# Attention's front and side work: load order, wide first projections, GpSimd norms and splits, paced pieces

## The chip, the cores and the metric

The kernel runs on one core of a Trainium2 chip. A core has TensorE (PE; its weight loads, PEld, are listed apart), VectorE (DVE), ScalarE (ACT), GpSimd (POOL) and SyncE (SP), which here only issues transfers. Each engine works through its own queue in order and waits for others by semaphores. The metric is the device time of one execution in microseconds, lower is better.

## The reference, cut to what matters

Two blocks of attention and feed-forward follow one another on x of shape (4, 1024, 128). The change touches the first attention alone, and the place in it where the first feed-forward's input is prepared:

```python
x = x + _L0_attn_ref(_layernorm(x), ...)      # 16 heads of 8, B=4, S=1024, E=128
...
Q = x @ wq + bq                               # and K, V
Q = Q.reshape(B * H, S, D)                    # a plain reshape: 64 groups of 1024 rows of 8
scores = einsum('bqd,bkd->bqk', Q, K) / sqrt(D)
ctx = einsum('bqk,bkd->bqd', softmax(scores), V)
out = ctx.reshape(B, S, E) @ wo + bo + x
out = (out - mean) * rsqrt(var + 1e-5) * gamma + beta
```

The reshape cuts the row-major result without a transpose, so a group of "Q" is 64 consecutive tokens x 16 chunks of 8 features. 512 tokens (a "half") hold eight such groups, treated as two sets of four.

## The kernel before, in words

**Stages.** `tile_block` loads x (`load_x`: eight transfers of 256 KB on SP), runs `attention` (0 to about 1001 us of the profile), the first feed-forward, a gated linear attention and a mixture of experts. Everything from `attention` on the engines other than PE is put into its queue by a scheduler that takes the earliest-written instruction that its model holds ready and whose buffer is free; PE's order in the main loop is the written one (`manual_schedule`).

**Front.** `attention` loads the weights wq and wk, then the biases bq and bk by 32 small transfers on ACT's queue (16 copies each, L250), then wv, wo, bv and three broadcast rows, then all weights of the later stages (`load_later_weights`, which also has DVE compute `half_s`, L83, from a loaded vector). `prepare(0)` then does the first half at once.

**prepare(hf)**, for each of the eight halves of 512 tokens: statistics of four 128-token tiles on DVE (`norm_stats`; the power -1/2 runs on GpSimd, L196), the scaling of each tile on DVE (`norm_apply`, L200), xnb = xn + bo on GpSimd (L311), four transposes (L318) and a copy to xnT on ACT (L319), then eight projections, four for k and four for q, of four chunks each: 16 small products into the one bank "misc" (L328; the profile lists 32 passes), the bias by DVE (`raw`, L336), and the signed split: hi = raw x sign, rounded, on DVE (L345), raw x take and the sum on GpSimd (L346, L347). `hi` and `raw` have two buffers each. Last `values` writes v (L366).

**The main loop** runs 16 sets x 2 query halves x 8 key chunks x 2 steps = 512 steps. A step has a score tile in a double bank (two products, L586, and two with the negated maxima, L595), its exponential on ACT (`pr`, L603), and a maxima tile for a later set: two products (L396) into a double bank and a reduction on DVE (`nm`, L403). The double banks come from one pool of three. Every second step adds the weighted sum (L513). The maxima lead by ten pairs of steps. When half a set's maxima are done, `place` splits them, GpSimd writes them into `mxpad` (L422, L423), and PE transposes them (L413) for the score tiles.

**Side work.** `others()` is called at every other step and takes one entry from `after` (places; and of a finished set: normalize L446 to L456, project, output, residual) and one from `ahead` (the next half's `prepare`), at most one of them with a use of "misc". When `ahead` is empty it also emits one of eleven comparison pieces of half 1 (`compare_pieces`, L120 to L123): four GpSimd operations over 512 columns on buffers of the tags `hi` and `raw`, which check the later weights. `output` adds the residual input (y) and has DVE take the statistics; `residual` scales on DVE (z, L200), after the power on GpSimd, and GpSimd does gamma, beta and the sum into x. In the last half `ahead` holds instead `first_pieces` (norm and transposes of the first two blocks for the feed-forward, xn in a `raw` buffer), the turning of the weights, and a flag.

Of the kernel before, what the change touches and what calls it, by code (L numbers as in the profile page):

```python
# [24 lines left out]
class Block:  # L25
# [5 lines left out]
    def __init__(self, ctx: ExitStack, tc: tile.TileContext, ins, out):  # L31
        self.tc, self.nc, self.ins, self.out = tc, tc.nc, ins, out
        nc = self.nc
        self.const = ctx.enter_context(tc.tile_pool(name="const", bufs=1))
        self.xs = self.ctile([P, NT, E], "xs")
        self.ident = self.ctile([P, P], "ident")
        make_identity(nc, self.ident)
        self.mhalf = self.ctile([P, 16], "mhalf")
        nc.gpsimd.memset(self.mhalf, -0.5)
# [4 lines left out]
    def load_x(self, x):  # L44
        src = x.rearrange("b s e -> (b s) e").rearrange("(n p) e -> p n e", p=P)
        h = TPB // 2
        for n in range(0, NT, h):
            self.nc.sync.dma_start(self.xs[:, n : n + h, :], src[:, n : n + h, :])
# [105 lines left out]
    def first_pieces(self, work, bank):  # L154

        nc, out = self.nc, []
        for blk, x2 in enumerate(self.first_x):
            src = self.xs[:, 4 * blk : 4 * blk + 4, :]
            got = {}

            def norm(src=src, got=got):
                mv, rs = self.norm_stats(work, src, 4)
                got["xn"] = xn = work.tile([P, 4, E], F32, name="xn", tag="raw")
                for k in range(4):
                    self.norm_apply(xn[:, k, :], src[:, k, :], mv, rs, k)

            def turn(x2=x2, got=got):
                ps = bank()
                for k in range(4):
                    nc.tensor.transpose(ps[:, k * P : (k + 1) * P], got["xn"][:, k, :], self.ident)  # L170
# [3 lines left out]
            out += [(0, norm), (1, turn)]  # L174
        return out[0::2] + out[1::2]
# [9 lines left out]
    def norm_stats(self, pool, src, n):  # L185
# [11 lines left out]
        return mv, rs  # L197

# [17 lines left out]
    def attention(self):  # L216
# [7 lines left out]
        with ExitStack() as ctx:  # L224
# [13 lines left out]
            wpad = {}  # L238
            for key in ("wq", "wk"):
                nat = ct([P, NC, D], f"{key}_nat")  # L240
                nc.sync.dma_start(nat, ins[f"L0_attn_{key}"].rearrange("i (c d) -> i c d", d=D))
                wp = ct([P, NC, 4, D], f"{key}_pad")
                nc.vector.tensor_copy(wp, nat.unsqueeze(2).to_broadcast([P, NC, 4, D]))
                wpad[key] = wp.rearrange("p c r d -> p c (r d)")
            b4 = {"wq": ct([P, NC], "bq4"), "wk": ct([P, NC], "bk4")}
            for key, bkey in (("wq", "bq"), ("wk", "bk")):
                src = ins[f"L0_attn_{bkey}"].rearrange("(c d) -> d c", d=D)
                with nc.allow_non_contiguous_dma(reason="128 words"):
                    for j in range(16):
                        nc.scalar.dma_start(b4[key][D * j : D * j + D, :], src)  # L250
# [22 lines left out]
            for cl in range(2):  # L273
                nc.scalar.dma_start(
# [4 lines left out]
            )  # L279
            self.load_later_weights()  # L280
# [13 lines left out]
            def prepare(hf):  # L294
# [10 lines left out]
                def stats():  # L305
                    got["ln"] = self.norm_stats(work, x_h, NT2)

                def apply():
                    for n in range(NT2):
                        self.norm_apply(xn[:, n, :], x_h[:, n, :], *got["ln"], n)  # L310
# [10 lines left out]
                def project(key, c0):  # L321
                    bt["done"].add((key, c0))
                    ps = misc()
                    ps3 = ps.rearrange("p (c n) -> p c n", c=4)
                    xj = xnT.rearrange("p (i j t) -> p j i t", j=4, t=T)
                    for cc in range(4):
# [8 lines left out]
                    raw = work.tile([P, 4, NSET, T], F32, name="raw", tag="raw")  # L335
                    nc.vector.tensor_tensor(  # L336
                        raw,
                        ps3.rearrange("p c (i t) -> p c i t", t=T),
                        b4[key][:, c0 : c0 + 4].unsqueeze(2).unsqueeze(3)
                        .to_broadcast([P, 4, NSET, T]),  # L340
                        ALU.add,
                    )

                    hi = work.tile([P, 4, NSET, T], F32R, name="hi", tag="hi")
                    nc.vector.tensor_scalar(hi, raw, sign[key], None, ALU.mult)  # L345
# [6 lines left out]
                    )  # L352

# [19 lines left out]
                todo = [(0, stats), (0, apply), (1, turn)]  # L373
                for k in ("wk", "wq"):
                    todo += [(1, lambda k=k, c=c: project(k, c)) for c in range(0, NC, 4)]
                todo += [(1, values)]
                bt["done"] = set()
                return bt, todo
# [57 lines left out]
            def finish(hf, i, qh, oacc, ctok, xnb):  # L436
# [6 lines left out]
                def normalize():  # L443
# [5 lines left out]
                    ps4 = ps.rearrange("p (c j r) -> p c j r", c=4, r=32)  # L449
                    rc = work.tile([P, 4, 4], F32, name="rc", tag="rc")  # L450
                    nc.vector.reciprocal(rc, ps4[:, :, :, D])
                    cv = ctok.rearrange("p h (q c l d) -> p q l c h d", q=2, l=2, d=D)
                    for cl in range(2):
                        rows = slice(cl * T, (cl + 1) * T)
                        for jl in range(2):
                            nc.vector.tensor_tensor(  # L456
                                cv[jl * T : (jl + 1) * T, qh, cl],
                                ps4[rows, :, jl::2, 0:D],
                                rc[rows, :, jl::2].unsqueeze(3).to_broadcast([T, 4, 2, D]),
                                ALU.mult,  # L460
                            )
# [9 lines left out]
                def output():  # L471
# [16 lines left out]
                    got["y"] = y  # L488
                    got["ln"] = self.norm_stats(work, y, 2)

                def residual():
                    y = got["y"]
                    z = work.tile([P, 2, E], F32, name="z", tag="z")
                    for h in range(2):
                        self.norm_apply(z[:, h, :], y[:, h, :], *got["ln"], h)
                    n0 = hf * NT2 + 2 * i
                    xt = xs[:, n0 : n0 + 2, :]

                    def row(t):
                        return t.unsqueeze(1).to_broadcast([P, 2, E])  # L500

                    nc.gpsimd.tensor_tensor(z, z, row(gamma_b), ALU.mult)
                    nc.gpsimd.tensor_tensor(z, z, row(beta_b), ALU.add)
                    nc.gpsimd.tensor_tensor(xt, xt, z, ALU.add)

                evacuate()
                after.append((1, normalize))
                if qh:
                    after.extend([(1, project), (1, output), (0, residual)])
# [27 lines left out]
            for _, f in todo:  # L537
# [10 lines left out]
            def others():  # L548


                free = True
                for queue in (after, ahead):
                    if queue and (free or not queue[0][0]):
                        banks, f = queue.popleft()
                        f()
                        free = free and not banks
                if free and not ahead and compare:
                    compare.pop(0)()

# [1049 lines left out]
```

## Time and profile before

| | us |
|---|---|
| median of 4 runs | 1651.91 (1640.6 to 1666.95) |
| the profiled execution | 1656.16 |
| its span, first to last instruction | 1654.4 |
| mean granted TensorE clock | 0.926 |

| engine | busy us | share | instructions |
|---|---|---|---|
| PE | 1397.5 | 84% | 10256 |
| DVE | 1111.4 | 67% | 1870 |
| ACT | 841.9 | 51% | 1056 |
| GpSimd | 483.9 | 29% | 462 |

Busy shares are averages over the stages, and a busy PE isn't a PE at its peak. A row of the timeline gives start, duration, engine, line, operation, what is written <- what is read, and in brackets the engine's idle time before it with what ended it. A wait for several semaphores is put down to the one that came last. The granted clock is a record of changes between 1.0 and 0.5, with none before 56 us.

### The profile page before, as it was taken

What the parts mean: (1) busy time and instruction counts of PE and PEld (TensorE: products, weight loads), DVE (VectorE), ACT (ScalarE), POOL (GpSimd) and SP (SyncE); (2) the same over time, 40 slices, a digit from 0 to 9 for tenths busy, and PEclk for the clock granted to TensorE, in tenths of its full rate; (3) what the DMA queues carried; (4) which work ended last, traced back from release to release, by engine and by line L of the source; (5) the groups of instructions that cost most, each with busy time, mean ns of one, the idle gap of its engine ahead of it and who ended that gap; (6) DMA issues with size and microseconds to landing.
All of it is one profiled execution on the core that took longest, in us unless ns stands there. A gap on an engine that the chain in (4) does not pass through costs nothing.

```text
span 1654.4 us, 25028 instructions
## 1 busy us (share of the span) xinstructions
PE 1397.5 (84%) x10256; PEld 706.4 (43%) x10256; DVE 1111.4 (67%) x1870; ACT 841.9 (51%) x1056; POOL 483.9 (29%) x462
## 2 busy tenths in 40 slices
PE   2699893889899898898988998988884878679998
PEld 1343341334343343343433434665652544445554
DVE  3798793799797798897987854777663555622220
ACT  0066652566655566566656675466663322254332
POOL 4442069036061060240430003554550000202110
PEclk9789997899997899999999998999995887789999
DMA  5000000000000000000000000000000000101110
GB/s 142 3 1 2 1 2 0 1 2 1 1 2 1 1 2 1 1 2 1 1 2 1 1 1 1 1 1 1 1 0 2 1 1 1 34 5 51 51 52 14
DMA packets 23247, 16.06 MB, mean 10 GB/s; under 512 B 9536, under 2 KB 20432, under 8 KB 23120
## 3 DMA queue, kind: packets, MB, share of 16 engines
q1 hardware_dynamic: 15792, 7.99, 1.7%
q0 software_dynamic: 1920, 6.29, 1.3%
q8 instruction: 84, 1.38, 0.3%
q10 hardware_dynamic: 5408, 0.05, 0.2%
q14 instruction: 43, 0.35, 0.1%
HBM read 12.23 MB, written 2.10 MB: 9 GB/s over the span
## 4 chain that ended last, share of the span: by engine, by line
PE 54%; DVE 22%; ACT 12%; issue 5%; POOL 5%; DMA 2%; ACTq 0%; SPq 0%; POOLq 0%; DVEq 0%
PE oacc L513 10%; DVE nm L403 10%; PE sc L586 7%; PE zT L1524 5%; PE mm L749 5%; PE up L1534 5%; PE mx L396 4%; ACT pr L603 4%; PE sc L595 3%; PE misc L328 2%; DVE raw L336 2%; ACT g L819 2%; DVE hi L345 1%; DVE att_s L1290 1%; POOL ln_rs L196 1%
## 5 line engine op out<-in xcount | busy, mean ns | idle before, releaser
L603 ACT ACTIVATE pr<-sc 128x1024 f32<-128x1024 f32 x512 | 518.4, 1026 | 351.0 <-PE sc L595 303.9
L403 DVE TENSOR_REDUCE nm<-mx 128x2 f32<-128x1024 f32 x512 | 614.5, 1219 | 110.7 <-PE sc L595 61.0
L396 PE MATMUL mx<-k,q 32*128 32x512 f32 x1024 | 267.2, 521 | 53.2 <-ACT pr L603 42.6
L586 PE MATMUL sc<-q,k 32*128 32x512 f32 x1024 | 255.2, 508 | 60.0 <-DVE nm L403 59.0
L513 PE MATMUL oacc<-pr,vaug 128*32 128x512 f32 x2048 | 284.7, 626 | 0.0
L586 PEld LDWEIGHTS sc<-q,k 32*128 32x128 f32 x1024 | 96.6, 187 | 333.4 <-DVE nm L403 135.7
L595 PE MATMUL sc<-mT,a_ones 32*128 32x512 f32 x1024 | 204.8, 399 | 0.0
L196 POOL TENSOR_TENSOR ln_rs<-ln_rs,mhalf 128x4 f32<-128x4 f32 (+2 forms) x44 | 42.9, 976 | 398.1 <-DVE ln_rs L195 397.8
L396 PEld LDWEIGHTS mx<-k,q 32*128 32x128 f32 x1024 | 98.4, 190 | 125.2 <-ACT pr L603 107.8
L1542 ACT ACTIVATE g<-up 128x512 f32<-128x512 f32 x96 | 56.7, 597 | 105.4 <-PE up L1534 105.3
L595 PEld LDWEIGHTS sc<-mT,a_ones 32*128 32x128 f32 x1024 | 99.8, 192 | 0.9 <-ACT mT L414 0.2
L1534 PE MATMUL up<-mT,wa 128*128 128x512 f32 x192 | 97.8, 600 | 0.4 <-DVE att_s L1290 0.4
L1524 PE MATMUL zT<-g,wb 128*128 128x512 f32 x192 | 97.5, 602 | 0.0
L422 POOL COPY mxpad<-mhi 128x16 f32<-128x16 f32 x32 | 6.8, 214 | 269.9 <-PE sc L595 239.0
L1534 PEld LDWEIGHTS up<-mT,wa 128*128 128x128 f32 x192 | 58.7, 310 | 31.8 <-issue 19.4
L513 PEld LDWEIGHTS oacc<-pr,vaug 128*32 128x32 f32 x2048 | 41.2, 109 | 72.5 <-issue 70.6
L826 POOL TENSOR_TENSOR g_lo<-g,g_hi 128x512 fp32r<-128x512 f32 x48 | 66.0, 1388 | 18.4 <-ACT g_hi L824 14.0
L346 POOL TENSOR_SCALAR raw<-raw,wk_take 128x512 f32<-128x512 f32 x32 | 50.2, 1568 | 67.1 <-DVE hi L345 67.1
L789 POOL TENSOR_TENSOR h_lo<-h,h_hi 128x512 fp32r<-128x512 f32 x32 | 44.4, 1389 | 41.9 <-ACT h_hi L788 41.9
L346 POOL TENSOR_SCALAR raw<-raw,wq_take 128x512 f32<-128x512 f32 x32 | 50.3, 1573 | 21.1 <-DVE hi L345 21.1
L1290 DVE TENSOR_TENSOR att_s<-att,cseen 128x1024 f32<-128x1024 f32 x32 | 38.4, 1220 | 20.7 <-PE att L1282 20.4
L328 PE MATMUL misc<-xnT,wk_pad 128*32 128x128 f32 x1024 | 38.0, 294 | 16.9 <-ACT xnT L319 14.4
(249 smaller groups left out, 2006.2 us busy)
## 6 DMA issues: line engine op xcount, KB each, us to landing
xs<-in_L_attn_x SPq DMA_DIRECT2D x8, 256.0 KB
h_nat<-in_L_ffn_h_w SPq DMA_DIRECT2D x2, 1024.0 KB
out<-xs SPq DMA_DIRECT2D x8, 256.0 KB
w_nat<-in_L_ffn_w_w SPq DMA_DIRECT2D x3, 256.0 KB
bq<-in_L_attn_bq ACTq DMA_DIRECT2D x16, 0.5 KB
bk<-in_L_attn_bk ACTq DMA_DIRECT2D x16, 0.5 KB
gWo<-in_L_attn_Wo SPq DMA_DIRECT2D x16, 4.0 KB
wa<-in_L_ffn_Wa,at_i POOLq DMA_INDIRECT x12, 3.6
```

The costliest lines, as they stand in the source:

```text
L328: nc.tensor.matmul(ps3[32 * j : 32 * j + 32, cc, :], wpad[key][:, c0 + cc, :], xj[:, j], start=True, stop=True,)
L346: nc.gpsimd.tensor_scalar(raw, raw, take[key], None, ALU.mult)
L396: nc.tensor.matmul(ps[:, jj, :], qf[32 * j : 32 * j + 32, ch * P : (ch + 1) * P], kf[32 * j : 32 * j + 32, kh * KH : (kh + 1) * KH], start ...
L403: nc.vector.tensor_reduce(nm[:, kh, ch, 2 * jp : 2 * jp + 2], ps, AX.X, ALU.max, negate=True)
L513: nc.tensor.matmul(pend["oacc"][32 * j : 32 * j + 32, :], pend["v"][:, j, pend["ch"], :], pend["p"][j // 2][:, j % 2, :], start=pend["ch"] ...
L586: nc.tensor.matmul(ps[:, jj, :], kf[rows, ch * P : (ch + 1) * P], qf[rows, qh * KH : (qh + 1) * KH], start=True, stop=False,)
L595: nc.tensor.matmul(ps[:, jj, :], ones[rows, :], mT[rows, qh * KH : (qh + 1) * KH], start=False, stop=True,)
L603: nc.scalar.activation(pr, ps, AF.Exp, scale=scale)
L749: nc.tensor.matmul(ps, wT[name][:, ic, oc * P : (oc + 1) * P], half, start=ic == 0 and h == 0, stop=ic == n_ic - 1 and h == 1,)
L826: eng.tensor_tensor(g2[1], g, g2[0].bitcast(F32), ALU.subtract)
L1524: nc.tensor.matmul(zT, zones[k][1][:, fc * E : (fc + 1) * E], g, start=n == 0, stop=n == len(steps) - 1,)
L1534: nc.tensor.matmul(ps, zones[k][0][:, fc, :], xT[:, hb * TB : (hb + 1) * TB], start=True, stop=True,)
```

## The change

1. **Loads.** One of x's eight transfers is issued before everything else, then wk, bk, wq, bq; the other seven come after the attention's small weights and before the later weights. The biases are loaded as rows of 16 x 8, repeated by DVE, and turned by one small product each. No transfer is issued on ACT's queue.
2. **First half.** Its four `project8` handle eight chunks each in a double bank of the score pool, with the rounding on ACT and the sum as two mixed products on DVE, in buffers of the exponentials' pool.
3. **Norms.** `norm_pieces` cuts a norm into statistics by two tiles, the power, and the scaling, which runs on GpSimd; used in `prepare`, in the residual and in `first_pieces`, whose xn gets buffers of its own.
4. **Splits.** For the other halves hi = raw x sign runs on GpSimd too.
5. **Pacing.** `others` is called at every step, work with a bank still at every other one; entries of `ahead` carry a gap in steps (four for a projection), and a comparison piece is emitted every six steps, whether `ahead` is empty or not. `normalize` leaves half of its divisions to a later call; the residual's statistics become an entry of their own.

```diff
+        self.load_x(ins["L0_attn_x"], 0, 1)
         make_identity(nc, self.ident)
...
+    def norm_pieces(self, pool, src, n, dst):
...
+        def gather():
+            for i in range(n):
+                nc.vector.bn_aggr(mv[:, i, :], st[:, i, :])
+            nc.vector.tensor_scalar(rs, mv[:, :, 1], EPS, None, ALU.add)
+            nc.gpsimd.tensor_tensor(rs, rs, self.mhalf[:, :n], ALU.pow)
+
+        def apply():
+            for i in range(n):
+                nc.gpsimd.tensor_scalar(
+                    dst[:, i, :], src[:, i, :], mv[:, i, 0:1], rs[:, i : i + 1],
+                    ALU.subtract, ALU.mult,
+                )
...
-                    for j in range(16):
-                        nc.scalar.dma_start(b4[key][D * j : D * j + D, :], src)
...
+                nc.vector.tensor_copy(wide, rows[key].unsqueeze(1).to_broadcast([NC, 16, D]))
...
+            self.load_x(ins["L0_attn_x"], 1, NT // NT2)
             self.load_later_weights()
...
-                    nc.vector.tensor_scalar(hi, raw, sign[key], None, ALU.mult)
+                    nc.gpsimd.tensor_scalar(hi, raw, sign[key], None, ALU.mult)
                     nc.gpsimd.tensor_scalar(raw, raw, take[key], None, ALU.mult)
...
+                def project8(key, c0):
+                    bt["done"] |= {(key, c0), (key, c0 + 4)}
+                    ps = ps_big.tile([P, 2 * KH], F32, name="pj", tag="big")
+                    ps, bias = products(ps, key, c0, 8)
+                    raw = expp.tile([P, 8, NSET, T], F32, name="raw8", tag="pr")
+                    nc.vector.tensor_tensor(raw, ps, bias, ALU.add)
+                    hi = expp.tile([P, 8, NSET, T], F32R, name="hi8", tag="pr")
+                    nc.scalar.activation(hi, raw, AF.Copy, scale=sign[key])
+                    for i in range(NSET):
+                        nc.vector.scalar_tensor_tensor(
+                            bt[key[1]][:, i, c0 : c0 + 8, :],
+                            raw[:, :, i, :],
+                            take[key],
+                            hi.bitcast(F32)[:, :, i, :],
+                            ALU.mult,
+                            ALU.add,
+                        )
...
+                else:
+                    todo += [(0, gather, 1), (0, apply, 3), (1, turn, 2)]
+                    for k in ("wk", "wq"):
+                        todo += [
+                            (1, lambda k=k, c=c: project(k, c), 4) for c in range(0, NC, 4)
+                        ]
...
-            def others():
-                free = True
-                for queue in (after, ahead):
-                    if queue and (free or not queue[0][0]):
-                        banks, f = queue.popleft()
-                        f()
-                        free = free and not banks
-                if free and not ahead and compare:
+            def others(free):
+                step[0] += 1
+                if after and (free or not after[0][0]):
+                    banks, f = after.popleft()
+                    f()
+                    free = free and not banks
+                if ahead and step[0] >= step[1] and (free or not ahead[0][0]):
+                    _, f, gap = ahead.popleft()
+                    step[1] = step[0] + gap
+                    f()
+                if compare and step[0] >= step[2]:
                     compare.pop(0)()
+                    step[2] = step[0] + 6
...
-                            else:
-                                others()
+                            others(jp == 0)
```

## The prediction

> **What bounds the kernel now.** I read the page's groups first, then the start of every exponential (the rows "pr<-sc") in the timeline, then the waits, the sums by 25 us, and the timeline of 0 to 130, 196 to 226 and 240 to 315 us. Attention lasts from 0 to about 1001 us of a span of 1654.4; the diff touches only this part, except that the first block's norm for the next layer is prepared inside it. The page's groups (line, engine, operation, tiles, shapes, count | busy us, mean ns | idle before):
>
> ```profile
> L603 ACT ACTIVATE pr<-sc 128x1024 f32<-128x1024 f32 x512 | 518.4, 1026 | 351.0 <-PE sc L595 303.9
> L403 DVE TENSOR_REDUCE nm<-mx 128x2 f32<-128x1024 f32 x512 | 614.5, 1219 | 110.7 <-PE sc L595 61.0
> ...
> L346 POOL TENSOR_SCALAR raw<-raw,wk_take 128x512 f32<-128x512 f32 x32 | 50.2, 1568 | 67.1 <-DVE hi L345 67.1
> ```
>
> Neither ACT nor DVE fills the stage. Two steps (one pair: two score tiles, two maxima tiles, one weighted sum) take 3.33 us almost everywhere; DVE's two maxima are 2.44 of that and ACT's two exponentials 2.05. All four tiles of a pair turn through three double banks, so the pair is a chain of fill, read, refill. 256 pairs x 3.33 = 852.5 us. The first exponential starts at 80.1 and the last ends at 999.6: 919.5. So 67 us of attention are excess over the beat, and 80 us pass before the beat begins; these two are what the change can reach. By sets of 16 pairs (floor 53.3) the excess is: set 0 4.2, sets 2, 4, 6, 8, 10 4.1, 4.1, 3.6, 3.2, 3.2, set 3 30.9, set 7 10.1, sets 12 and 13 3.5 and 2.6, the other odd ones 0.5 to 1.9, and set 15 is 7 below.
>
> Set 3 is one event. The sums by 25 us show it (columns: the stretch, its length, busy us and instructions of PE, PEld, DVE, ACT, GpSimd, then the granted clock, the DMA share and GB/s), then the waits (who waits for whom: us in total, times, longest) and the timeline (start, us, engine, line, and the idle time before with its releaser):
>
> ```profile
> 250.00:275.00 25.00, 14.15 (x104) 5.16 (x98) 12.59 (x19) 9.82 (x11) 25.00 (x24) 0.85 0.00 1
> 275.00:300.00 25.00, 8.76 (x40) 2.81 (x40) 8.11 (x10) 3.99 (x4) 16.09 (x17) 0.50 0.00 0
> ```
> ```profile
> DVE z L200 <- POOL ln_rs L196: 37.2, 16, 24.7
> ...
> ACT L319 <- DMA bk<-in_L_attn_bk: 29.6, 1, 29.6
> ...
> PEld misc L413 <- POOL mxpad L423: 5.1, 6, 3.8
> ```
> ```profile
> 262.31 1.62 DVE L195 TENSOR_SCALAR ln_rs<-ln_mv 128x2 f32<-128x2 f32 x1
> ...
> 286.68 1.26 POOL L123 TENSOR_TENSOR same<-same,eq 128x512 f32<-128x512 f32 x1
> 287.90 0.73 POOL L196 TENSOR_TENSOR ln_rs<-ln_rs,mhalf 128x2 f32<-128x2 f32 x1
> 288.66 0.60 DVE L200 TENSOR_SCALAR z<-y,ln_mv,ln_rs 128x128 f32<-128x128 f32 x2 [24.73 <-POOL ln_rs L196]
> ```
>
> GpSimd runs the eleven comparison pieces in one go (244 to 288), the power of a norm is queued behind them, and DVE, whose next instruction scales with that power, stands for 24.7 us with all maxima behind it. PE and ACT stop, and the clock is granted at 0.5 from 267.6 to 305, so the next pairs take 4.99, 4.99 and 4.53.
>
> **The front.** ACT's queue first issues 32 tiny bias loads; the copy that starts the projections waits for the last (29.58), the eight projections follow about 2.8 us apart, each on the one bank "misc", and the maxima that lead by ten pairs end near 76.4.
>
> ```profile
> 29.58 1.28 ACT L319 ACT_TABLE_LOAD   x1 [29.58 <-DMA bk<-in_L_attn_bk]
> ...
> 31.52 1.94 PE L328 MATMUL misc<-xnT,wk_pad 128*32 128x128 f32 x32 [14.42 <-ACT xnT L319]
> ...
> 33.52 0.69 DVE L336 TENSOR_TENSOR raw<-misc,bk 128x512 f32<-128x512 f32 x1 [6.22 <-PE misc L328]
> ...
> 59.49 15.91 DVE L403 TENSOR_REDUCE nm<-mx 128x2 f32<-128x1024 f32 x14
> ...
> 80.06 1.02 ACT L603 ACTIVATE pr<-sc 128x1024 f32<-128x1024 f32 x1 [1.00 <-PE sc L595]
> ```
>
> **Part 1, front.** The 32 loads become two on SP, ahead of seven of the eight x loads. The power of the first norm ended at 7.5 us before; its x load landed at 4.1 and can't land later when it goes first and alone. Then four normalizations on GpSimd: no such row; its 512-wide multiply is 1.57, its 256-wide adds 0.73, so a quarter of 1.57 to 0.6 each, I take 0.45: 1.8. Transposes 1.25, copy 0.59: xnT at 11.3. Weights and bias rows, issued between 2 and 5 us, landed 3.0 to 3.8 us after issue elsewhere (bo_b, wq), so by 9: hidden. A wide projection is two of 1.94 = 3.9 on PE, alternating between three free banks; then DVE 1.22 (the maxima read as much), ACT 1.02, DVE two mixed products of 0.75 (as L803, x512). Maxima need three wide ones: 11.3 + 11.7 + 1.2 + 1.0 + 1.5 = 26.7. Then on DVE sixteen maxima x 1.13 (15.91/14) = 18.1, the fourth projection's 2.7 and values 0.7: 48.2; from the sixteenth maximum to the first exponential 3.6 as before: 52. To that I add 1 of a possible wait of 0 to 6: half_s (L83) on DVE waits for a scale vector whose load now stands behind the x loads; before, DVE stood there 6.4 us and it cost nothing, because ACT was later. So 53 instead of 80: -27 (-22 to -31).
>
> The clock is at stake here. The projections' 32 matmuls took 1.94 at 31 to 48 us and 1.08 after 93.6, where the granted clock is 1.0; with pauses of 0.8 us between them they never sped up. "TensorE: Matmul & The Clock Gate", Part 1, says that about 3.4 us of sustained work releases the clock; by that the later wide projections would take 2.2, and the front would be up to 3 us shorter. No row here has so long an early run, so the sum keeps 3.9.
>
> **Part 2, set 3.** z's scaling moves to GpSimd, so no DVE instruction waits for a power any more, and the pieces are emitted six steps (10 us) apart. All 30.9 go: -31. Against it, GpSimd's load while half 2 is prepared: a projection costs it 1.57 + 1.57 + 1.31 = 4.45 (2.88 before), 56 of them +88 us in all. Eight per half are 35.6, eleven pieces at 3.9 (43/11) 43, two residuals (0.73 + 0.9 + 3 x 0.73 = 3.8) 7.6, a norm and xnb 4, places 1.8: 92 of 107 us. In its first 44 steps (73 us), 64 us of work come due: a lag of some microseconds. Behind a lag stand DVE's raw (two buffers shared by projections and pieces) and PE's transposes of mxpad. Nothing lost to 20 us lost; I take +6, nearer to the free end, because before, at 2.88 us of GpSimd per 3.33, the transposes waited only 5.1 us in six cases.
>
> **Part 3, even sets.** Pairs 4 to 7 of an even set take 3.8, 5.0, 4.0, 3.9. At 203 to 214 DVE does y, statistics, waits 0.82 for the power, scales z 0.60, scales xn 1.46 + 0.59 (two each; the first two slow beside GpSimd), a new aggregation, and the split's hi. Scaling, wait and hi (64 x 0.54) leave DVE; projections come 6.7 us apart instead of 3.3. The rest (2.44 + about 0.5 a pair) fits under 3.33. Of 18.2 I take 12; of the odd sets' pair 4 (0.47 each) 3; of sets 12 and 13 4, since there DVE's xn waited 1.22 for a buffer shared with the splits, and has its own now. Sum -19 (-8 to -25).
>
> Here a page speaks against the change: "GPSIMD Engine Reference", 3.1, calls GpSimd about 2x slower than the Vector engine at elementwise work and says to leave that on the latter. By 2x a moved split would be 1.0 us. The trace is worse (1.57 against 0.54), but GpSimd idles 71% of the span, so the price is only paid where something waits for it.
>
> **Part 4, what is added on the path.** DVE's small operations can wait for GpSimd (L195 took 1.62 once, usually 0.17; L345 up to 1.60), and GpSimd is busier; mxpad may stand behind 4.45 instead of 2.88 us of a split, with 3.3 us between place and transpose. +4 (0 to 12). Calls of the queue at both steps of a pair issue no extra work. Half-clock stretches without a long stall (520.2, 27 us, costing 10) I neither add nor remove.
>
> Sum: -27 -31 + 6 -19 + 4 = -67. The profiled run took 1656.2 (1.8 around the span) and lies 4.2 above the median: 1656.2 - 67 - 4.2 = 1585.
>
> **Rivals.** (a) GpSimd becomes the bound, slower than before: if its lag at a place exceeds the 3.3 us that the transpose leaves it, PE stops, at up to 32 places. Each would have to cost 2.1 us to eat the 67, and 2.6 us (83) to be slower by 1%: one more 1.57 us instruction plus half clock in one of the record's 3.4 us units (1.7 lost) is 3.3, in all 105: about 1690. For it: six such waits exist already, the longest, 3.8, in the front. Against: outside half 2 GpSimd has 49 us to do per 107. (b) The front isn't shortened, DVE standing at half_s or at statistics of x that lands late while the projections wait: first exponential near 76; -67 + 23: 1608. For it: DVE stood at half_s from 16.6 to 23.0. (c) The comparison's stall comes back through raw's buffers or mxpad, 25 us: 1610. For it: the pieces run whenever they are free to, not where they are emitted (the first cast ran at 244.1, before the last projections' products). (b) and (c) together: 1633, at the edge of no change. That the change leaves both losses untouched has nothing for it.
>
> **Numbers.** Forecast 0.62, (b) 0.11, (c) 0.12, both 0.06, (a) 0.09. A measurement can tell about 1% (16.5 us). Faster by over 1%: forecast, (b), (c): 0.85; within: 0.06; slower: 0.09. The forecast's own bounds: front -31 and -22, set 3 -31 and -11, Part 3 -25 and -8, Part 4 0 and +12; all together 1565 and 1623. To take in (b) and (c) with a little loss besides, 1562 to 1628.
>
> **What would show it.** First exponential at 49 to 58; no row "z <- POOL ln_rs" on DVE; no window with GpSimd at 25 of 25 and PE under 15; set 3 under 62 us; pairs 5 to 7 of even sets under 3.6; GpSimd's busy time up by 90 to 110, DVE's down by about 60. Wrong if PE waits at mxpad over 30 us in all, if DVE waits for a DMA between 12 and 50 us, or if the half-clock stretches between 100 and 1000 us sum to more than the 75 of before.

## The result: no change, and the profile after

| | before | after |
|---|---|---|
| median, us | 1654.88 (78 runs, 1640.6 to 1684.38) | 1655.66 (52 runs, 1649.46 to 1675.39) |
| ratio | | 1.0016, 95% interval 1.0003 to 1.0029 |
| profiled execution, its span, us | 1656.16, 1654.4 | 1657.01, 1654.8 |
| mean granted clock | 0.926 | 0.917 |
| start of the first exponential, end of the last, us | 80.06, 999.57 | 64.44, 999.60 |
| time at half clock between 100 and 1000, us | 75 | 92 |
| busy us of PE, DVE, ACT, GpSimd | 1397.5, 1111.4, 841.9, 483.9 | 1398.1, 1074.1, 846.9, 604.0 |

The forecast of 1585, and its range of 1562 to 1628, are missed. The large change moved work, and the time stayed: the beat of attention begins 15.6 us earlier and ends where it ended. Medians are over all runs of a kernel, while ratios and their intervals take only the runs within 1.5% of its fastest, so a ratio can differ a little from the quotient of two medians. (The median of 4 runs that the prediction started from, 1651.9, lay 3 us below that of 78.)

Where it went is read from the first exponential of every set of 16 pairs, in us (the beat alone takes 53.3):

| set | 0 | 1 | 2 | 3 | 4 | 5 | 6 | 7 | 8 | 9 | 10 | 11 | 12 | 13 | 14 | 15 |
|---|---|---|---|---|---|---|---|---|---|---|---|---|---|---|---|---|
| before | 57.5 | 53.8 | 57.4 | 84.2 | 57.4 | 53.8 | 56.9 | 63.4 | 56.5 | 55.2 | 56.5 | 53.9 | 56.8 | 55.9 | 53.8 | 46.4 |
| after | 61.8 | 66.2 | 68.3 | 62.9 | 64.7 | 53.4 | 61.7 | 53.4 | 69.4 | 53.4 | 59.2 | 53.4 | 53.8 | 53.7 | 53.3 | 46.5 |

Gained: the front 15.6, set 3 21.3, set 7 10.0, sets 12 and 13 5.2, sets 5, 9, 11 and 14 together 3.2: 55.3. Given back: sets 0, 1, 2, 4, 6, 8 and 10 4.3 + 12.4 + 10.9 + 7.3 + 4.8 + 12.9 + 2.7 = 55.3. What follows is about these 55 us.

The groups of the page after, in the columns of before (L470 and L682 are the old L403 and L603; the third was DVE's before):

```profile
L470 DVE TENSOR_REDUCE nm<-mx 128x2 f32<-128x1024 f32 x512 | 623.5, 1222 | 157.4 <-PE sc L674 91.3
L682 ACT ACTIVATE pr<-sc 128x1024 f32<-128x1024 f32 x512 | 516.8, 1025 | 347.9 <-PE sc L674 288.3
...
L381 POOL TENSOR_SCALAR hi<-raw,wk_sign 128x512 fp32r<-128x512 f32 x28 | 43.9, 1568 | 82.8 <-DVE raw L379 82.8
```

The work on the main beat is what it was; DVE's idle time ahead of the maxima grew from 110.7 to 157.4 us, although DVE has 37 us less to do. GpSimd's moved work waits in its turn for DVE (82.8). Neither row says what holds the beat up; the waits further down do. The same 25 us stretches of set 3 as before:

```profile
250.00:275.00 25.00, 20.84 (x216) 9.30 (x214) 21.02 (x25) 15.42 (x17) 24.75 (x22) 1.00 0.01 1
275.00:300.00 25.00, 19.79 (x206) 9.27 (x200) 14.99 (x20) 11.10 (x12) 24.36 (x25) 0.80 0.00 1
```

GpSimd, the fifth sum, is full in both (24.75 and 24.36 of 25, where it had 25.00 and 16.09), while PE now works 20.84 and 19.79 us where it had worked 14.15 and 8.76. That stall is gone, as forecast: set 3 fell from 84.2 to 62.9. The waits, though, have new rows. These are DVE's and then PE's on GpSimd:

```profile
DVE lp_mv L210 <- POOL xn L216: 36.4, 7, 6.8
```
```profile
PE misc L480 <- POOL mxpad L490: 29.4, 13, 9.3
...
PE misc L353 <- POOL xn L216: 11.8, 4, 10.8
```

At mxpad the row of PE before, and that of its weight loads (PEld) after, are:

```profile
PE misc L413 <- POOL mxpad L423: 3.3, 1, 3.3
```
```profile
PEld misc L480 <- POOL mxpad L490: 34.9, 14, 9.6
```

The 37.2 us of "z <- POOL ln_rs" are gone. In their place DVE's **aggregation** of statistics waits 36.4 us for GpSimd's scaling, and PE waits 29.4 us at the transposes of mxpad, where it had waited 3.3. The prediction's 5.1 for this wait is the row of PEld, which grew to 34.9.

**The first of these** in the timeline of set 2 (start, us, engine, line, and in brackets the idle time before it):

```profile
210.33 0.80 POOL L216 TENSOR_SCALAR xn<-xs,lp_mv,lp_rs 128x128 f32<-128x128 f32 x1
211.09 0.72 POOL L574 TENSOR_TENSOR xs<-xs,z 128x256 f32<-128x256 f32 x1
211.79 2.35 POOL L216 TENSOR_SCALAR xn<-xs,lp_mv,lp_rs 128x128 f32<-128x128 f32 x3
214.18 0.38 DVE L210 BATCH_NORM_AGGREGATE lp_mv<-lp_st 128x2 f32<-128x6 f32 x4 [6.83 <-POOL xn L216]
...
216.13 0.79 PE L665 MATMUL sc<-q,k 32*128 32x512 f32 x2 [6.08 <-DVE nm L470]
```

Norms have two buffers of statistics, taken in turn. The four scalings on GpSimd here (210.33 to 214.14) are those of the fourth half and read one of them; the aggregation of the sixth half, whose own scaling comes some 250 us later (459.6), writes into that buffer. The scheduler had put it into DVE's queue as soon as its model held the buffer free, and in the queue it stands ahead of maxima that the main loop wants. GpSimd is late, as the four scalings stand behind a residual's operations. DVE stands for 6.83 us, PE for 6.08. It happens four times at 6.8 us in the main loop (214, 345, 463, 579 us) and once at 2.6; the other two are in the front. The four pairs with 6.8 us take 11.3, 11.3, 11.0 and 13.2 us, where the same pairs of sets 2, 4, 6 and 8 had taken 5.0, 5.0, 5.0 and 4.8: 27 us in all, with a further wait of 3.3 us for GpSimd in the last. The scaling's own price, from one line's view (least, median and longest ns):

```profile
L216 POOL TENSOR_SCALAR xn<-xs,lp_mv,lp_rs x32: 783/798/815, 18.7 to 700.5; 128x128 f32<-128x128 f32 x32
```

So four of them are 3.15 us, not the 1.8 of the forecast; on DVE, in the first experiment below, they took 0.35 each (326, 354, 444), 1.1 to 1.4 for four.

"GPSIMD Engine Reference", section 3.1, of the Trainium skill measures GpSimd at about twice the Vector engine's time for an add of two inputs of 2048 elements. For this scaling, which reads one tensor of 128 elements per partition, it is 0.798 to 0.354 here, 2.3 times.

**The second**, at the start of set 1:

```profile
155.61 1.49 POOL L124 TENSOR_SCALAR eq<-eq 128x512 f32<-128x512 f32 x1
157.19 1.26 POOL L125 TENSOR_TENSOR same<-same,eq 128x512 f32<-128x512 f32 x1
...
158.54 0.23 POOL L490 TENSOR_TENSOR mxpad<-least,mhi 128x16 f32<-128x16 f32 x1
...
158.82 1.12 PE L480 MATMUL misc<-ident,mxpad 128*128 128x128 f32 x4 [9.31 <-POOL mxpad L490]
```

L122 to L125 are the comparison's pieces. They are emitted six steps apart from set 2 on, which begins at 192 us, but the scheduler took the first two into GpSimd's queue ahead of that, in one go between a projection's splits (they begin at 146.4 and 152.5), and the two small writes into mxpad (L489, L490) come behind all of it. PE's next instruction is the transpose: 9.31 us. In the 10 us from 150 on PE works 1.18 us and the granted clock is 0.60; the pair with the stop takes 14.6 us and the next 4.99, before the clock rises again. Smaller ones follow at 226.5 (2.83), 290.1 (4.77), 593.6 (1.98) and 706.2 (3.39).

**The front**, where the second x load has landed at 16.2:

```profile
7.70 1.05 POOL L212 TENSOR_TENSOR lp_rs<-lp_rs,mhalf 128x4 f32<-128x4 f32 x1 [1.43 <-DVE wq_wide L276]
...
17.64 1.01 POOL L212 TENSOR_TENSOR lp_rs<-lp_rs,mhalf 128x4 f32<-128x4 f32 x1 [8.89 <-DVE lp_rs L211]
...
18.66 3.15 POOL L216 TENSOR_SCALAR xn<-xs,lp_mv,lp_rs 128x128 f32<-128x128 f32 x4
...
21.84 0.38 DVE L210 BATCH_NORM_AGGREGATE lp_mv<-lp_st 128x2 f32<-128x6 f32 x4 [2.93 <-POOL xn L216]
...
23.01 6.62 PE L361 MATMUL pj<-xnT,wk_pad 128*32 128x128 f32 x128 [0.68 <-ACT xnT L354]
...
24.28 3.15 POOL L216 TENSOR_SCALAR xn<-xs,lp_mv,lp_rs 128x128 f32<-128x128 f32 x4
...
27.46 0.38 DVE L210 BATCH_NORM_AGGREGATE lp_mv<-lp_st 128x2 f32<-128x6 f32 x4 [3.51 <-POOL xn L216]
...
29.63 2.34 DVE L396 TENSOR_TENSOR raw<-pj,wk_b 128x1024 f32<-128x1024 f32 x2
```

The first half's power was done at 8.75 and its scaling could have followed, but GpSimd's queue held the power of the second half ahead of it (17.64), and that one's statistics need the second x load. Then DVE, at 21.84 and 27.46, stands at aggregations of the third and fourth halves behind GpSimd's scalings of the first and second, so that the first products, on PE from 23.01, are read at 29.63.

### The profile page after: what moved, and what is told of

It is laid out like the page before. It is cut to its first block, busy times and chain, and to the rows that moved or that the text cites. A ratio compares the mean times of both kernels' runs of the same rounds, so it can differ in the third digit from the quotient of the medians.

```text
span 1654.8 us, 25009 instructions
## 1 busy us (share of the span) xinstructions
PE 1398.1 (84%) x10260; PEld 711.2 (43%) x10260; DVE 1074.1 (65%) x1742; ACT 846.9 (51%) x1060; POOL 604.0 (37%) x574
## 4 chain that ended last, share of the span: by engine, by line
PE 56%; DVE 13%; ACT 11%; POOL 11%; issue 4%; DMA 0%; POOLq 0%; ACTq 0%; DVEq 0%
PE oacc L586 11%; PE sc L665 8%; PE zT L1601 5%; PE mm L826 5%; DVE nm L470 5%; PE up L1611 5%; ACT pr L682 4%; PE mx L463 4%; PE sc L674 3%; PE misc L361 2%; ACT g L896 2%; POOL z L216 1%; DVE ctok L525 1%; PE misc L480 1%; DVE att_s L1367 1%
## 5 line engine op out<-in xcount | busy, mean ns | idle before, releaser
L470 DVE TENSOR_REDUCE nm<-mx 128x2 f32<-128x1024 f32 x512 | 623.5, 1222 | 157.4 <-PE sc L674 91.3
L682 ACT ACTIVATE pr<-sc 128x1024 f32<-128x1024 f32 x512 | 516.8, 1025 | 347.9 <-PE sc L674 288.3
L463 PE MATMUL mx<-k,q 32*128 32x512 f32 x1024 | 269.9, 526 | 61.2 <-ACT pr L682 49.8
L194 POOL TENSOR_TENSOR ln_rs<-ln_rs,mhalf 128x4 f32<-128x4 f32 (+1 forms) x18 | 21.2, 1176 | 231.7 <-DVE ln_rs L193 231.6
L489 POOL COPY mxpad<-mhi 128x16 f32<-128x16 f32 x32 | 6.8, 212 | 192.7 <-PE sc L674 129.8
L381 POOL TENSOR_SCALAR hi<-raw,wk_sign 128x512 fp32r<-128x512 f32 x28 | 43.9, 1568 | 82.8 <-DVE raw L379 82.8
L212 POOL TENSOR_TENSOR lp_rs<-lp_rs,mhalf 128x2 f32<-128x2 f32 (+1 forms) x26 | 21.9, 844 | 104.3 <-DVE lp_rs L211 102.7
L381 POOL TENSOR_SCALAR hi<-raw,wq_sign 128x512 fp32r<-128x512 f32 x28 | 43.9, 1568 | 22.6 <-DVE raw L379 22.6
L1601 PEld LDWEIGHTS zT<-g,wb 128*128 128x128 f32 x192 | 36.5, 193 | 34.4 <-issue 24.9
```

The lines of the kernel that those rows point to most:

```text
L381: nc.gpsimd.tensor_scalar(hi, raw, sign[key], None, ALU.mult)
L463: nc.tensor.matmul(ps[:, jj, :], qf[32 * j : 32 * j + 32, ch * P : (ch + 1) * P], kf[32 * j : 32 * j + 32, kh * KH : (kh + 1) * KH], start ...
L470: nc.vector.tensor_reduce(nm[:, kh, ch, 2 * jp : 2 * jp + 2], ps, AX.X, ALU.max, negate=True)
L682: nc.scalar.activation(pr, ps, AF.Exp, scale=scale)
L1601: nc.tensor.matmul(zT, zones[k][1][:, fc * E : (fc + 1) * E], g, start=n == 0, stop=n == len(steps) - 1,)
```

## The experiments

The theory had three places, and each was to be cured by itself: the buffers of statistics that GpSimd's scaling gives back late; the writes into mxpad that stand behind splits and pieces; and in the front, work of later halves that is queued ahead of the first. The rival explanation was GpSimd's load as a whole: 120 us more work, whatever its order. All ratios are to the kernel before, with 95% intervals.

**The norms of `prepare` scaled on DVE.**

```diff
-                nc.gpsimd.tensor_scalar(
+                (by or nc.gpsimd).tensor_scalar(
                     dst[:, i, :], src[:, i, :], mv[:, i, 0:1], rs[:, i : i + 1],
...
-                stats, gather, on_pool = self.norm_pieces(work, x_h, NT2, xn)
+                stats, gather, on_pool = self.norm_pieces(work, x_h, NT2, xn, nc.vector)
```

> The changed kernel with one part undone: prepare's scaling of xn runs on DVE again, z's and first_xn's stay on GpSimd. Theory A (a new wait took the old one's place: DVE's aggregation of a later half stands until GpSimd has scaled the half whose statistics buffers it reuses, 6.8 us in sets 2, 4, 6 and 8, and the clock falls to half after it): the rows 'DVE lp_mv <- POOL xn' (36.4 us) vanish, the sixth pair of sets 2, 4, 6, 8 falls from 11 to 13 us to under 5.5, and the time is 30 to 42 us below the changed kernel's 1655.7, about 1620. Rival R (GpSimd is simply too busy, 604 us against 484, and its lateness shows up at the next engine that needs it): GpSimd loses about 25 us, and the waits move to mxpad and raw; the time falls by less than 15. The front should gain no more than 3 us, since the first scaling still stands behind statistics that wait for the second x load.

Measured: 1629.64, ratio 0.979 (0.969 to 0.989). The row "lp_mv <- POOL xn" is gone, and sets 0, 4, 6 and 10 are at 56.1, 55.6, 55.3 and 54.2. PE's waits at mxpad are still there (28.9 us). So 26 us went, less than the 30 to 42 expected, with a scaling that costs DVE more work, not less. The profiled execution shows beside it what a single stop at mxpad, 9.31 us at the same place, can cost. Sums by 10 us (length; PE, PEld, DVE, ACT, GpSimd with their counts; granted clock, DMA share, GB/s):

```profile
140.00:150.00 10.00, 0.97 (x4) 0.71 (x4) 1.02 (x1) 0.83 (x1) 8.80 (x10) 0.57 0.01 2
150.00:160.00 10.00, 9.26 (x45) 3.24 (x44) 4.30 (x4) 4.74 (x6) 0.00 (x0) 0.50 0.00 0
...
200.00:210.00 10.00, 10.00 (x48) 3.53 (x47) 5.80 (x10) 4.21 (x6) 0.00 (x0) 0.52 0.01 2
210.00:220.00 10.00, 9.75 (x100) 4.20 (x99) 9.83 (x24) 6.41 (x7) 6.81 (x8) 1.00 0.00 0
```

The clock falls at the stop (half from 141.3) and is back only at 209.6: set 1 takes 78.3 us. In the runs of this kernel that are on record the shortest is 1611.94, 18 less than the other three (1629.6 to 1629.7).

**More buffers for the statistics, the scaling left on GpSimd.**

```diff
-        st = pool.tile([P, n, 6], F32, name="lp_st", tag=f"ln_st{n}")
-        mv = pool.tile([P, n, 2], F32, name="lp_mv", tag=f"ln_mv{n}")
-        rs = pool.tile([P, n], F32, name="lp_rs", tag=f"ln_rs{n}")
+        st = pool.tile([P, n, 6], F32, name="lp_st", tag=f"ln_st{n}", bufs=10)
+        mv = pool.tile([P, n, 2], F32, name="lp_mv", tag=f"ln_mv{n}", bufs=10)
+        rs = pool.tile([P, n], F32, name="lp_rs", tag=f"ln_rs{n}", bufs=10)
```

> The changed kernel with ten instead of two buffers for the statistics, means and powers of a norm; every instruction stays on its engine, so GpSimd's busy time is the same 604 us. Theory A: the wait is for a buffer and nothing else; 36.4 us of 'DVE lp_mv <- POOL xn' go to under 3, and the time is about 1615 (1610 to 1628). Rival R: GpSimd's load is unchanged, so the time stays within 10 us of 1655.7. The front may be 0 to 4 us later, because all norms' powers are then queued early.

Measured: 1639.42, ratio 0.988 (0.984 to 0.992). The profile is of an execution of 1650.62, 11 us above that median, so only its waits are read here. GpSimd's work is the same (603.0 us) and the time falls by over 1%: load alone can't be the cause. But about half of the 40 us expected is missing, and DVE's waits show a new one:

```profile
DVE lp_st L206 <- POOL xs L574: 15.4, 4, 4.5
```

With buffers to spare the scheduler takes the next thing that it can early: the statistics of the blocks for the feed-forward, which wait for a residual's sum on GpSimd, up to 4.5 us at a time. PE still waits 26.8 us at mxpad. Here the stall came from an early place in a queue, and it moved when one of its conditions was lifted.

**mxpad written by DVE.**

```diff
-                    nc.gpsimd.tensor_copy(mp4[:, :, :, 0], hi.bitcast(F32))
-                    nc.gpsimd.tensor_tensor(
+                    nc.vector.tensor_copy(mp4[:, :, :, 0], hi.bitcast(F32))
+                    nc.vector.tensor_tensor(
                         mp4[:, :, :, 1], least, hi.bitcast(F32), ALU.subtract
```

> The changed kernel with the two small writes of mxpad on DVE instead of GpSimd. Theory B (PE's transposes of mxpad stand behind GpSimd's splits, norms and comparison pieces: waits of 9.3, 2.8, 4.8, 2.0 and 3.4 us in the main loop, each with a stretch of half clock): 'PE misc <- POOL mxpad' vanishes, sets 1 and 3 fall from 66.2 and 62.9 to under 57, set 10 to under 56, DVE's busy time rises by about 10 us, and the time is 25 to 35 us lower, about 1625. Rival: DVE then writes mxpad late itself, behind its own stand at lp_mv, and the gain is under 12. The stalls at lp_mv stay (sets 2, 4, 6, 8).

Measured: 1632.40, ratio 0.984 (0.975 to 0.993). PE's waits for GpSimd at mxpad are gone, sets 1, 3 and 10 fall to 53.4, 59.4 and 53.8, half clock falls from 92 to 65 us, and the 36.8 us of "lp_mv <- POOL xn" stay, with sets 4, 6 and 8 at 61.8, 65.9 and 67.1. The two waits are separate.

**The changed kernel without the comparison's pieces.** This one leaves out the test of the later weights.

```diff
                     if hf == 1:
-                        compare.extend(self.compare_pieces(work))
+                        pass
```

> The changed kernel without the eleven comparison pieces (it leaves out the test that the later weights are exact in the rounded format; the flag then always says that they are, which holds for these inputs). GpSimd does about 52 us less, all of it in halves 0 and 1. If the comparison's place in GpSimd's queue is what makes PE wait in sets 1 to 3 (theory B in part): sets 1 and 3 at 54 to 56, set 2 at 62 to 64, time 20 to 30 us lower, about 1630. If the pieces were harmless there (rival: the splits alone make GpSimd late): less than 8 us. Sets 4, 6, 8 and 10 don't change in either case.

Measured: 1629.88, ratio 0.983 (0.975 to 0.991). Sets 1 and 3 are at 53.4, the waits at mxpad fall to 11.7 us, the 36.7 us at the statistics stay. So the pieces are what holds mxpad up in sets 1 to 3; the waits that remain there are of 0.3 to 0.4 us.

**The kernel before without the same pieces**, the test left out in the same way:

> The kernel before without the comparison pieces (it leaves out the test of the later weights' exactness). This prices the one stall that the prediction gave 31 us: DVE's z behind the power behind the pieces. Expected: no wait of over 2 us at z, set 3 at 54 to 58 instead of 84.2, and 24 to 32 us less than before: 1623 to 1630. If the stall is not the pieces' doing, nothing changes.

Measured: 1621.64, ratio 0.979 (0.970 to 0.988). Set 3 falls from 84.2 to 53.9, and the stretches that began the prediction read:

```profile
250.00:275.00 25.00, 22.07 (x160) 8.32 (x158) 20.92 (x30) 15.89 (x18) 3.29 (x6) 1.00 0.00 1
275.00:300.00 25.00, 21.37 (x166) 8.00 (x166) 19.68 (x22) 15.41 (x17) 0.38 (x2) 1.00 0.00 1
```

Set 3's 30.3 us confirm the size of the forecast's second term, 31, by themselves. (Set 7 falls too, from 63.4 to 53.9: the half-clock stretch at 520 us isn't in this profile.) The last two runs also set the scale: of the pieces' 49 us of GpSimd's busy time (483.9 to 434.7 here), on an engine that is mostly idle, the kernel before pays 33 us in one stop and the changed one 26 in several.

**All three of these on DVE**: the scalings of `prepare` and of `first_pieces` (with `nc.vector` passed to `norm_pieces` there as well) and mxpad's writes.

> Both undoings together on the changed kernel: the scaling of xn and of first_xn and the writes of mxpad run on DVE; z's scaling, the splits and the comparison stay on GpSimd. If the two waits (lp_mv behind the scaling, mxpad behind GpSimd's queue) are separate and are what ate the gain, the savings add: 28 (norm alone) + 25 (places alone) under the changed kernel's 1655.7, with sets 2 to 11 all at 53.4 to 57 and half clock between 100 and 1000 us under 40: 1595 to 1605. If GpSimd's load is the cause (rival), a third wait, DVE's raw behind the splits, takes their place: over 1620.

Measured: 1590.91, ratio 0.959 (0.952 to 0.966). This is 64.8 below the changed kernel's 1655.66. The single savings (26.0 and 23.3) add up to 49.3; the other 15 no run takes apart, but set 8, where the norms of `first_pieces` run, falls from 69.4 to 59.7, and half clock is 41 us in place of 92. Sets 2, 3 and 8 (59.4, 57.7, 59.7) stay above the 57 expected. GpSimd is still busy for 561.9 us, 78 more than before the change.

**The split's hi back on DVE**, in the changed kernel and in the last one:

```diff
-                    nc.gpsimd.tensor_scalar(hi, raw, sign[key], None, ALU.mult)
+                    nc.vector.tensor_scalar(hi, raw, sign[key], None, ALU.mult)
```

> The changed kernel with only the split's hi on DVE again (56 operations of 1.57 us off GpSimd, 604 to about 516 us busy, and 56 of 0.5 us back on DVE). Theory: the stalls hang on which short operation stands in which queue, not on load; lp_mv's waits stay at 25 to 36 us, since scaling and residual are still queued on GpSimd, and only those at mxpad shrink: 10 to 25 us below the changed kernel, about 1638. Rival (GpSimd's load is the cause): with nearly the old load both kinds of wait go, and the time comes under 1620.

> Norms, mxpad and the split's hi all on DVE; of the change remain the front, the paced side work, z's scaling and the wide first projections. It tells what the moved split is worth where nothing waits for GpSimd. If GpSimd's 88 us are hidden there and DVE has room for 27 us (sets at 53.4 leave it 0.3 to 0.9 us a pair), the time is the 1591 of the kernel with the split on GpSimd within 6. Rival 1: DVE is full in the sets with projections, and it is 8 to 20 slower. Rival 2: the late splits still cost in sets 2 and 3 (59.4 and 57.7), and it is 4 to 8 faster.

Measured in the changed kernel: 1646.28, ratio 0.993 (0.990 to 0.997). It takes 84 of the 120 added us off GpSimd (519.8 busy), more than any edit above. The wait at the statistics stays, and that at mxpad is smaller (29.4 before this edit):

```profile
DVE lp_mv L210 <- POOL xn L216: 36.7, 7, 6.8
```
```profile
PE misc L480 <- POOL mxpad L490: 16.9, 4, 8.0
```

The time falls by 9 us only. It doesn't settle the matter alone, as the same edit gives DVE 22 us more to do, but the rows do: without most of the added load the first wait is all there, and so is more than half of the second. The rival, load whatever its order, falls with that; load has a part in the second wait. In the kernel with the three repairs the same edit makes the time longer: 1607.89, ratio 0.971 (0.963 to 0.978) against 0.959, with four runs each that don't overlap (1595.1 to 1611.0 against 1585.6 to 1592.7); sets 0, 4, 6 and 10 go from 56.1, 55.1, 55.1 and 53.7 to 60.1, 59.1, 59.2 and 58.0, DVE's busy time from 1097.0 to 1119.6. So the moved split was worth some 17 us, once GpSimd's results were not waited for elsewhere.

**The front: x's other loads earlier**, in the changed kernel and in the one with the three repairs:

```diff
                 )
+            self.load_x(ins["L0_attn_x"], 1, NT // NT2)
             for key in ("wk", "wq"):
...
-            self.load_x(ins["L0_attn_x"], 1, NT // NT2)
             self.load_later_weights()
```

> The changed kernel with that one move of the seven x loads. First exponential at 54 to 58 instead of 64.4 if the second half's power is what the first scaling waits for; over 62 if not. The rest of attention keeps its stalls, so the time falls by no more than 10.

> The same, and the other seven x loads are issued right after wk, bk, wq and bq, ahead of wv, wo, bv and the broadcast rows. In the changed kernel the first scaling stood from 8.8 to 18.7 us because GpSimd's queue holds the second half's power before it, and that waits for the second x load (landed at 16.2). If that order is the front's loss, the first exponential comes at 52 to 56 instead of 60 to 64, and the time is 5 to 9 us below the same kernel with late x loads. Rival: the front is bound by the four wide projections and the twenty maxima, and the first exponential moves by less than 2.

Both missed. In the changed kernel the first exponential moves only from 64.4 to 62.3 (1655.21, ratio 1.001, 0.996 to 1.006); with the repairs from 60.1 to 59.1 (1592.32, ratio 0.959, 0.951 to 0.966). The timeline of the first of the two shows what comes next:

```profile
14.42 6.54 PE L361 MATMUL pj<-xnT,wk_pad 128*32 128x128 f32 x128 [0.68 <-ACT xnT L354]
...
19.93 1.27 POOL L435 TENSOR_TENSOR xnb<-xn,bo_b 128x512 f32<-128x512 f32 x1 [6.72 <-DMA bo_b<-in_L_attn_bo]
...
25.35 0.38 DVE L210 BATCH_NORM_AGGREGATE lp_mv<-lp_st 128x2 f32<-128x6 f32 x4 [10.75 <-POOL xn L216]
...
27.51 2.34 DVE L396 TENSOR_TENSOR raw<-pj,wk_b 128x1024 f32<-128x1024 f32 x2
```

The projections run 8.6 us earlier than in the changed kernel, but xnb on GpSimd waits for the broadcast row bo, which now lands at 19.9; behind it stand the power and the scaling of the second half, and behind those DVE's aggregation, for 10.75 us. The products of 14.42 are read at 27.51. In the other kernel DVE waits 7.28 us for the same xnb.

**The row bo and the two scale vectors too, ahead of the x loads**, on top of that:

```diff
+            bo_b = self.row_bcast(ins["L0_attn_bo"], "bo_b")
...
+                self.early_s = {
+                    n: self.load(ins[f"L0_ffn_{n}_s"].rearrange("(c p) -> p c", p=P), f"{n}_s")
+                    for n in ("w1", "w2")
+                }
             self.load_x(ins["L0_attn_x"], 1, NT // NT2)
```

> The kernel with norms and mxpad on DVE and the early x loads, and bo and the two scale vectors of half_s are loaded ahead of the seven x loads as well. In the run with early x alone the projections began 8.6 to 9.5 us earlier but DVE then stood 7.3 us on a norm of the second half that waited for GpSimd's xnb, which waited for bo (landed at 19.1), and half_s came before the bias additions too. If these waits in line are all that holds the front, the first bias addition starts at 17 to 20 instead of 24.4, the first exponential at 52 to 55, and the time is 4 to 8 us below the 1591 to 1592 of its two forerunners. If the front is bound elsewhere (rival), the first exponential stays at 58 to 60.

Measured: 1583.41 (1580.40 to 1587.07), ratio 0.9585 (0.9544 to 0.9625). The timeline of its front:

```profile
11.87 1.10 DVE L216 TENSOR_SCALAR xn<-xs,lp_mv,lp_rs 128x128 f32<-128x128 f32 x4
...
14.18 4.70 PE L367 MATMUL pj<-xnT,wk_pad 128*32 128x128 f32 x128 [0.68 <-ACT xnT L360]
...
17.86 2.33 DVE L402 TENSOR_TENSOR raw<-pj,wk_b 128x1024 f32<-128x1024 f32 x2
```
```profile
52.58 1.02 ACT L688 ACTIVATE pr<-sc 128x1024 f32<-128x1024 f32 x1 [1.00 <-PE sc L680]
```

No engine waits more than 0.2 us for a load between 11.87 and 52.5, the products are read as PE ends them (17.86), and the first exponential starts at 52.6, which is the forecast's 53. This kernel and the one with the three repairs beat both kernels of the case by about 4%. Between these two the ratios (0.9585 and 0.9589) settle nothing; the profiled executions show 7.5 us at the first exponential and 4.5 at the last.

## Why the prediction was wrong, step by step

- **What bounds the kernel; set 3.** Right. The 31 us are there, and nothing but the pieces makes them (53.9 without). The wait at z is gone, as forecast; what z's move and what the pacing of the pieces did to it, no run separates. Set 3 kept 9.6 us over the beat, with the stop of 4.77 at mxpad in it.
- **"So no DVE instruction waits for a power any more", and Part 3's "Scaling, wait and hi (64 x 0.54) leave DVE".** True of a power of z, and here is the step that failed: no new wait of DVE was put in for xn's scaling on GpSimd. The prediction follows that scaling to its reader (the transposes, in Part 1) and not to the next writer of what it reads. DVE's aggregation waits for it, 36.4 us in place of 37.2, in the even sets, where the forecast had counted a gain (of 18.2 us "I take 12"). Sets 0, 2, 4, 6, 8 and 10 lost 42.9 us, 27 of them in the four pairs with these waits; some of the rest is mxpad's (2.83 in set 2, 1.98 in set 8, 3.39 in set 10). The three repairs bring these sets to between 53.7 and 59.7.
- **The scaling's price.** 0.45 taken, from 0.39 to 0.6 as bounds; 0.80 measured. A 512-wide row of one operation, divided by four, doesn't price a 128-wide row of two; how much of the 0.80 is a fixed cost, no run separates. Four are 3.15, not 1.8.
- **"+6 for GpSimd's lag" and Part 4's +4.** The place was right, the size was not: PE waits 29.4 us at mxpad, 3.3 of them in the front. Set 1, ahead of the preparation of half 2 for which the forecast counted its lag, has the longest stop and lost 12.4, since the pieces' six steps hold where they are emitted and not where they run. The forecast's 3.9 us a piece is low too: nine of the eleven ran between 244 and 288 before, the other two at 385.7 and 392.2, and all eleven keep GpSimd busy for 49.8 us, 4.5 each. The stops bring half clock, which the forecast had neither added nor removed (92 us for 75). Rivals (a) and (c), 0.21 together without (c)'s share of the joint case, named this mechanism; (a) priced it at 32 places of 3.3 us, 105 in all, where there were 13 waits, and (c) priced it alone, at 25, as one stall. The cases were taken one at a time with the rest of the gain intact. What came was a part of each, of (b) too, and a wait that was in none.
- **The front, -27.** -15.6 measured. In the last experiment its 53 is met (52.6), but partly by luck: there DVE does the scaling, the projections start at 14.18 where the sum had 11.3, and the first two take 4.70 where it had 7.8. In the changed kernel its cover failed: the forecast named half_s as the wait that might come, and it cost little (DVE reaches it at 29.31, after the aggregation). The queue orders weren't read: powers of later halves ahead of the first scaling, aggregations ahead of the products, bo ahead of the second half. Rival (b) has "statistics of x that lands late while the projections wait": half of its price came.
- **The wide projections.** The 3.9 us each, PE cold, were the careful end. Two took 6.62 (128 passes), and the next 86 passes 2.57, 1.9 for 64. So PE did speed up within some 6 us of steady work (from 23.01; the clock's record has 1.0 from 29.0). It moved nothing, since DVE read them late.
- **Parts that held.** Loads of biases and weights hidden; sets 12 and 13 gained 5.2 for 4, and the odd sets 5, 9 and 11 2.6 for 3; hi on GpSimd worth some 17 us where nothing waits for it.
- **Not in the forecast.** Set 7's 10.0 us are the half-clock stretch at 520 us (27 us long) that the profile before has and the one after hasn't. Whether the change took it away or that one execution had it by chance, no run tells.
- **"What would show it."** Right: no DVE row waits for a power of z. Missed: first exponential 64.4 (49 to 58), set 3 62.9 (under 62), pairs 5 to 7 of even sets (11.3, 3.3 and 7.7 in set 2, under 3.6), GpSimd's busy time up by 120 (90 to 110), DVE's down by 37 (60). Of the three signs that would make it wrong, two came: DVE waits for the second x load up to 16.16, 7.28 us, and half clock is 92 (over 75). The third, over 30 us at mxpad, is at 29.4 by the row of PE and came by that of PEld (34.9), from which the prediction had its 5.1. "GpSimd at 25 of 25 and PE under 15" is met by no stretch of 25 us between 100 and 350; the stops are shorter than that.

What stays open: how long a half-clock stretch lasts after a stop was seen and not explained (after the 9.3 us stop at mxpad it began at 151.9 and lasted 17.1 us in the changed kernel, and began at 141.3 and lasted 68.3 in the first experiment). The 18 us between that experiment's runs may come from it; no profile of its fastest run shows it.

## What to carry to other kernels

When work moves to a slower engine, list not only who reads its result but who may overwrite its inputs, and what a scheduler has already queued behind that release: an idle share of 71% says nothing about a buffer that comes free late, here 6.8 us, for an instruction at the head of an in-order queue. Move what has no reader or writer waiting on the beat (the wide splits), and keep the short operations whose completion frees something (a 0.35 us scaling, a write of 16 columns) on the engine that needs them next. In a front, write down each queue in order: here powers of later halves, bo and the scale vectors, none of them needed first, stood ahead of the first projections' readers (the first exponential at 64.4 with them there, at 52.6 without, where the scaling was on DVE too).

## What was not expected of the hardware

In the first experiment PE was busy 85 to 100% of every 10 us from 150 to 210, by its modelled ends, while the clock was granted at 0.5 (rows above for the first and the last of these six). "TensorE: Matmul & The Clock Gate", Part 1, of the Trainium skill lets a busy window of about 3.4 us release the clock; the front's projections (steady from 23.01, full clock from 29.0) agree with that, these 60 us don't, and the measurement decides.
